# First attention of a two-layer transformer: where values and the output's last product stand in an iteration, and the order of the program's beginning

## The chip, the core and the metric

The kernel runs on one core of a Trainium2 chip. The core has five engines with a queue of instructions each: TensorE (PE; its loads of stationary operands are shown as PEld), VectorE (DVE), ScalarE (ACT), GpSimd (POOL) and SyncE (SP), which issues most DMAs. The metric is the device time of one execution in microseconds (us). The profile comes from one profiled execution; its span runs from the first to the last instruction.

## The reference

```python
x = x + xattn0(layernorm(x), fside, ctx, ctx)   # 16 heads of 8; 128 keys from fside, 120 from ctx
x = x + moe0(layernorm(x))                      # top 2 of 8 experts, silu
x = x + xattn1(layernorm(x), ctx, ctx)          # 16 heads of 8; 120 keys
x = x + moe1(layernorm(x))                      # top 2 of 8 experts, gelu
```

x is [64, 128, 128] in float32: 64 batches of 128 rows of width 128. An attention computes q, k and v with weights and biases, softmax(q k^T / sqrt(8)) v per head, and a product with the output weight. In the first one, the keys and values are 128 rows made from fside with the layer's weights, and 120 rows of ctx taken as they are. `moe0` makes its routing logits with a small attention over the eight experts' q, k, v.

## The kernel before

**Work and stages.** The 64 batches stay in SBUF as `xg`, in 16 groups of four (GB = 4). The program is: the first attention (to about 600 us), the first experts in 71 tiles of 256 tokens (to about 840), the second attention with the second experts beside it. The change is in the first attention and in what comes before it.

**An iteration of the first attention** (the loop in `attention`, from L482). It is a software pipeline: iteration `it` computes maxima for batch `it`, scores for batch `it - 2`, values and the first steps of the output for batch `it - 3`, and the last product for `it - 4`. Its parts, with the names used here:

- *Rounds* (`round_`, four per iteration, called in two pairs). Each has two maximum banks and two score banks of PSUM. A maximum bank (L344) is q k^T with queries on the partitions; DVE reduces it to the negated row maximum `nm` (L356). A score bank (L372) is k q^T; ACT takes its exponential into `p` (L380). The four matmuls of a bank pair use different groups of 32 rows of PE and run beside each other. A round issues the first half of all four banks, then the second.
- *Shift* (`shift`): PE transposes `nm` (L401), and DVE adds it to the queries (L404, two updates), so that scores come out with the maximum subtracted. Shift is for batch `it - 1`, and the next iteration's scores read the result.
- *Values* (`values`, L417): 32 matmuls p v into one bank, and `out1`, a copy of it by ACT (L426).
- *out2*: two transposes (L433), reciprocal of the sums (L437) and the product `o` (L439) on DVE. *out3*: a transpose (L446) and a copy on ACT (L448). *out4*: the product with wo (L453). *out5*: DVE adds to x (L458), and takes the statistics for the next normalisation (L113).
- *Preparation* (`prep`) of the group to come, spread over four iterations: queries (L269, and four ACT activations L273, two at each of the two places of `prep`), keys (L187, two activations L192), values (L199, DVE L206), and turning the normalised x (L165, ACT copy L166).
- *Router* (`aside.call`, twice in an iteration): small steps of the first experts' routing, on DVE (L655 to L806), PE, ACT and POOL, with the scatter DMAs of tokens on POOL (L754). Its `front` normalises a group on POOL (L156), turns it on PE and makes logits (L618), at times that `when` sets in iterations.
- *Lead* (`aside.ahead`): statistics of x for a group some ten batches ahead.

The order of a full iteration is: values and out1; DMA loads; rounds 0 and 1; out2; first part of preparation; rounds 2 and 3; shift; out3; router; out4 and out5; lead; second part of preparation; router.

**What sets the order.** The loop is recorded under `tc.manual_schedule`, so each engine executes in the order of the code. All PSUM tiles of this attention come from one pool of eight banks (`mtile`), so a new one waits until the last reader of an older one is done. What precedes the loop (constants, loads, first keys, values and queries) is recorded outside of it, in an order that a scheduler chooses. SP issues DMAs in order and waits at each for the one eight before.

**The beginning.** Four loads of x are issued first, then masks, the layer's weights, constants of the router, then fside's group 0 (`kvT`), the context's keys and values, and the other twelve loads of x. Group 0 is normalised on POOL and turned, and its queries are made for four batches at once.

Of the kernel before, what the change touches and what calls it, by code (L numbers as in the profile page):

```python
# [8 lines left out]
F32 = mybir.dt.float32  # L9
# [35 lines left out]
def transformer_kernel(ctx, tc, a, out):  # L45
# [16 lines left out]
    for g in range(4):  # L62
        load_x(g)
# [14 lines left out]
    def attention_weights(p):  # L78
        return dict(
            wq=load_const(p + "wq", [D, D], a[p + "wq"]),  # L80
            wk=load_const(p + "wk", [D, D], a[p + "wk"]),
            wv=load_const(p + "wv", [D, D], a[p + "wv"]),
            wo=load_const(p + "wo", [D, D], a[p + "wo"]),
            bq=load_const(p + "bq", [128, NS], a[p + "bq"]),
            bk=load_const(p + "bk", [128, NV], a[p + "bk"]),
            bv=load_row(p + "bv", D),
            bo=load_row(p + "bo", D),
        )

    hmask = load_const("hmask", [128, NS], a["hmask"])  # L90
    kmask = load_const("kmask", [128, NV], a["kmask"])
    smask = load_const("smask", [128, NV], a["smask"])
    l0 = attention_weights("a0_")
# [5 lines left out]
    class Norm:  # L99
# [6 lines left out]
        def stats(self, b):  # L106
            if self.n < 2:

                if b % GB == 0:
                    self.halves[b // GB] = stat.tile(  # L110
                        [S, GB, 6], F32, name=f"st{self.n}", tag=f"st{self.n}", bufs=3
                    )
                nc.vector.bn_stats(self.halves[b // GB][:, b % GB, :], xg[b // GB][:, b % GB, :])  # L113
                return
            st = stat.tile([S, 6], F32, name="st", tag="st")
            nc.vector.bn_stats(st, xg[b // GB][:, b % GB, :])
            nc.vector.bn_aggr(self.mv[:, b, :], st)  # L117

# [31 lines left out]
        def normed(self, g, pool=rows, bufs=1, width=D, xn=None, js=range(GB)):  # L150

            if xn is None:
                xn = pool.tile([S, GB, width], F32, name="xn", tag="xn", bufs=bufs)
            for j in js:
                b = g * GB + j
                nc.gpsimd.tensor_scalar(  # L156
                    xn[:, j, :D], xg[g][:, j, :], self.mv[:, b, 0:1], self.rstd[:, b : b + 1],
                    ALU.add, ALU.mult,
                )
            return xn  # L160
# [13 lines left out]
    for s in range(2):  # L174
        k = keep.tile([128, NV, GB, KF + KC], F32, name=f"k2_{s}", tag=f"k2_{s}")
        K2.append(k)
        v = keep.tile([KF, GB, H // 2, 2, 32], F32, name=f"v_{s}", tag=f"v_{s}")
        nc.gpsimd.memset(v, 0.0)
        for i in range(2):
            nc.gpsimd.memset(v[:, :, :, i, 16 * i + HD : 16 * i + HD + 1], 1.0)  # L180
        VS.append([v])
        m = keep.tile([S, 2, 128], F32, name=f"nm_{s}", tag=f"nm_{s}")
        nc.gpsimd.memset(m, 0.0)
        NM.append(m)
# [32 lines left out]
    def attention(layer, w, norm, first, aside):  # L217
# [5 lines left out]
        with ExitStack() as es:  # L223
# [18 lines left out]

            def context(g):
                if first:
                    s = g % 2
                    for v in range(NV):
                        nc.sync.dma_start(
                            k2[s][:, v, :, KF:], a["ctx_k"][:, v, g * GB : (g + 1) * GB, :]
                        )
                    nc.sync.dma_start(  # L250
                        vs[s][1].rearrange("k b h i w -> k b (h i w)"),
                        a["ctx_v"][:, g * GB : (g + 1) * GB, :],
                    )
# [49 lines left out]
            def prep(it, half):  # L303

                g, j = it // GB + 1, it % GB
                if not first:
                    if g == 1:
                        if (j, half) == (2, 1):
                            prep_v(1)
                        elif (j, half) == (1, 0):  # L310
                            prep_k(1)
                    elif g < NG:
                        pieces = (
                            (), (lambda: prep_k(g),),
                            (lambda: prep_v(g), lambda: prep_x(g)),
                            (lambda: prep_q(g, 0), lambda: prep_q(g, 1)),
                        )[j]
                        if half < len(pieces):
                            pieces[half]()
                    return  # L320
                if (it, half) == (0, 1):
                    norm_of(1)
                    prep_x(1)
                if (j, half) == (3, 1):
                    if g + 1 < NG:
                        prep_x(g + 1)
                elif g >= NG:
                    return
                elif j == 0 and it or it == 1:
                    prep_q(g, half)  # L330
                elif (j, half) == (2, 0):
                    prep_k(g)
                elif (j, half) == (2, 1):
                    prep_v(g)
# [126 lines left out]
            def norm_of(g):  # L461
                if g < NG:
                    normed[g] = norm.normed(g)

                    nc.gpsimd.tensor_tensor(
                        xg[g], xg[g], w["bo"].unsqueeze(1).to_broadcast([S, GB, D]), ALU.add
                    )

            if first:
                loads(0)  # L470
                context(0)
                yield
                norm_of(0)
                prep_k(0)
                prep_v(0)
                prep_x(0)
                prep_q(0, 0)
                prep_q(0, 1)
            else:
                prep_batch(0)  # L480
            loads(1)
            oTs, pos_ = {}, {}  # L482

            for it in range(B + (4 if first else 5)):
# [17 lines left out]
                on(3, lambda b: values(b, 0), lambda b: values(b, 1), out1)  # L502
# [3 lines left out]
                if it % GB == 2 and it // GB + 1 < NG:  # L506
                    context(it // GB + 1)
                rounds(0, 1)
                if first:

                    on(3, out2)
                    prep(it, 0)
                    rounds(2, 3)
                    on(1, shift)
                    on(3, out3)
                    aside.call(it, mtile)
                    on(4, out4, out5)
                    aside.ahead(it)
# [3 lines left out]
                else:  # L522

# [15 lines left out]
                    if it == 1:  # L539

                        nc.gpsimd.tensor_tensor(
                            xg[0], xg[0], w["bo"].unsqueeze(1).to_broadcast([S, GB, D]), ALU.add
                        )
# [18 lines left out]
    class Router:  # L562
# [5 lines left out]
        def __init__(self, pool, layer, norm, nlog, wr, logits, chosen, xnT_of, parts, when=(7.5, 8)):  # L568
# [145 lines left out]
    def logits1(rt, lg, n, l):  # L714
# [19 lines left out]

    spare = nc.sync.dma_start(
        xs[E * CAP - TT :].rearrange("(h p) d -> p h d", p=S),
        zero,
    )
    AFTER = mybir.DependencyInfo(mybir.DependencyClass.Sync, mybir.DependencyReason.DATA)
    DEEP = 4  # L740
    scatters = []
# [5 lines left out]
    def scatter(probe, j, k, xn):  # L747
# [11 lines left out]
        behind(s, [scatters[-DEEP] if len(scatters) >= DEEP else spare])  # L759
# [317 lines left out]
    class Aside0(Ahead):  # L1077
# [12 lines left out]

        def made(self, b):
# [17 lines left out]
    wr0 = load_const("wqkvT", [D, 3 * E], a["wqkvT"])  # L1109
# [3 lines left out]
    rp = ctx.enter_context(tc.tile_pool(name="route", bufs=1))  # L1113
    aside0 = Aside0()
    steps = attention(0, l0, norms[0], True, aside0)
    next(steps)
    for b in range(GB):
        aside0.lead(b)
    next(steps)
# [251 lines left out]
```

## Time and profile before

| | |
|---|---|
| three runs | 1531.78 us median, 1529.79 to 1535.51 |
| profiled execution | 1534.94 us, span 1533.1 us |
| mean granted TensorE clock | 0.976 |
| PE busy | 1415.5 us (92%) |
| DVE busy | 1057.7 us (69%) |
| ACT busy | 836.7 us (55%) |
| POOL busy | 641.6 us (42%) |
| first matmul of a round | 21.66 us |
| eight iterations, 195.19 to 268.59 us | 73.40 us |

A row of the timeline gives the start, the duration, engine, line, operation, output and inputs with their shapes and types, and a count when rows are merged; in brackets stands the idle time before it and what ended it. A row of the windows gives a stretch, its length, busy time and instructions of PE, PEld, DVE, ACT and POOL, the granted clock of PE as a share of full speed, the busy share of the DMA engines, and GB/s. A row of the waits gives who waited for whom: total us, times, longest. PE's ends are modelled, so time in which a block of matmuls waits inside counts as busy; distances between starts of blocks are safer.

### The profile page before, as it was taken

What the parts mean: (1) busy time and instruction counts of PE and PEld (TensorE: products, weight loads), DVE (VectorE), ACT (ScalarE), POOL (GpSimd) and SP (SyncE); (2) the same over time, 40 slices, a digit from 0 to 9 for tenths busy, and PEclk for the clock granted to TensorE, in tenths of its full rate; (3) what the DMA queues carried; (4) which work ended last, traced back from release to release, by engine and by line L of the source; (5) the groups of instructions that cost most, each with busy time, mean ns of one, the idle gap of its engine ahead of it and who ended that gap; (6) DMA issues with size and microseconds to landing.
All of it is one profiled execution on the core that took longest, in us unless ns stands there. A gap on an engine that the chain in (4) does not pass through costs nothing.

```text
span 1533.1 us, 44848 instructions
## 1 busy us (share of the span) xinstructions
PE 1415.5 (92%) x18156; PEld 1148.4 (75%) x18156; DVE 1057.7 (69%) x2923; ACT 836.7 (55%) x1722; POOL 641.6 (42%) x1211
## 2 busy tenths in 40 slices
PE   5999999999999999888999997579999999999988
PEld 3777777777777777777888887457787777777765
DVE  4777888888888986454544443458777767777763
ACT  3766666666666655433333332346666666656643
POOL 5123255656565635543000000677755565544110
PEclk9999999999999999999999999689999999999999
DMA  7421122222222221467766665111111111110000
GB/s 191 113 54 49 48 59 62 66 62 62 63 62 62 57 72 43 152 183 213 206 196 184 197 195 145 36 34 29 36 33 29 36 38 34 34 29 22 9 12 25
DMA packets 124130, 123.89 MB, mean 81 GB/s; under 512 B 47123, under 2 KB 106515, under 8 KB 122003
## 3 DMA queue, kind: packets, MB, share of 16 engines
q1 hardware_dynamic: 115730, 103.71, 24.8%
q0 software_dynamic: 8192, 17.32, 3.6%
q8 instruction: 143, 2.34, 0.6%
q14 instruction: 65, 0.52, 0.1%
HBM read 97.31 MB, written 23.67 MB: 79 GB/s over the span
## 4 chain that ended last, share of the span: by engine, by line
PE 67%; DVE 15%; POOL 6%; DMA 5%; ACT 4%; issue 3%; SPq 1%; POOLq 0%; ACTq 0%; DVEq 0%
PE bank L372 12%; PE bank L417 10%; PE bank L344 9%; PE bank L1000 9%; DVE nm L356 5%; PE bank L1228 4%; PE bank L1249 3%; PE bank L1013 3%; DMA q<-xs 2%; DMA vc<-xs 2%; PE bank L433 2%; DVE q L404 2%; PE bank L618 2%; PE bank L187 2%; DVE h L1243 2%
## 5 line engine op out<-in xcount | busy, mean ns | idle before, releaser
L356 DVE TENSOR_REDUCE nm<-bank 128x2 f32<-128x496 f32 (+1 forms) x768 | 461.9, 662 | 105.9 <-PE bank L372 74.2
L372 PE MATMUL bank<-q,k 32*120 32x256 f32 (+1 forms) x3072 | 452.3, 406 | 7.2 <-DVE q L404 4.4
L380 ACT ACTIVATE p<-bank 120x512 f32<-120x512 f32 (+1 forms) x768 | 401.1, 602 | 105.2 <-PE bank L372 70.4
L344 PE MATMUL bank<-k,q 32*128 32x248 f32 (+1 forms) x4096 | 449.1, 340 | 2.4 <-ACT q L298 1.1
L344 PEld LDWEIGHTS bank<-k,q 32*128 32x128 f32 x4096 | 347.4, 188 | 63.7 <-issue 21.7
L372 PEld LDWEIGHTS bank<-q,k 32*120 32x120 f32 (+1 forms) x3072 | 291.4, 181 | 36.6 <-DVE nm L356 17.0
L1005 DVE TENSOR_TENSOR p<-p,bank 128x256 f32<-128x256 f32 x213 | 88.4, 420 | 134.1 <-ACT p L1004 134.1
L417 PE MATMUL bank<-p,v 128*32 128x128 f32 (+1 forms) x4096 | 177.9, 279 | 0.1
L754 POOL DMA_INDIRECT xs<-xn,at x128 | 128.8, 1006 | 52.8 <-issue 29.5
L1160 POOL DMA_INDIRECT yb<-ys,back x128 | 123.7, 967 | 32.5 <-issue 25.7
L1004 ACT ACTIVATE p<-bank 128x256 f32<-128x256 f32 x213 | 81.0, 383 | 100.7 <-PE bank L1000 100.2
L426 ACT COPY ov<-bank 128x256 f32<-128x256 f32 x128 | 47.8, 373 | 158.7 <-PE bank L417 158.7
L417 PEld LDWEIGHTS bank<-p,v 128*32 128x32 f32 (+1 forms) x4096 | 110.3, 110 | 20.3 <-issue 12.3
L1000 PE MATMUL bank<-q 128*128 128x256 f32 x516 | 118.6, 379 | 1.8 <-ACT q L991 1.8
L404 DVE SCALAR_TENSOR_TENSOR q<-bank,c_smask,q 128x256 f32<-128x256 f32 x256 | 111.2, 476 | 11.8 <-PE bank L401 9.0
L156 POOL TENSOR_SCALAR xn<-x,mv,rstd 128x128 f32<-128x128 f32 x256 | 111.2, 447 | 11.6 <-PE bank L165 5.7
L273 ACT ACTIVATE q<-bank,c_a_bq,c_hmask 128x512 f32<-128x512 f32 x124 | 89.7, 780 | 29.0 <-PE bank L269 29.0
L417 PE MATMUL bank<-p,vc 120*32 120x128 f32 x2048 | 104.6, 274 | 0.3 <-issue 0.3
L1000 PEld LDWEIGHTS bank<-q 128*128 128x128 f32 x516 | 94.7, 190 | 13.2 <-ACT q L991 2.1
L1146 POOL MEMSET gates<- 128x256 f32 x2 | 0.6, 312 | 248.4 <-DMA ys<-q 248.4
L144 POOL TENSOR_SCALAR rstd<-mv 128x4 f32<-128x4 f32 (+1 forms) x33 | 6.5, 197 | 202.7 <-DVE mv L117 113.7
L1000 PE MATMUL bank<-vc 128*128 128x256 f32 x336 | 78.8, 385 | 0.0
(201 smaller groups left out, 2271.1 us busy)
## 6 DMA issues: line engine op xcount, KB each, us to landing
q<-in_w SPq DMA_DIRECT2D x43, 576.0 KB, 4.4
vc<-in_w SPq DMA_DIRECT2D x28, 576.0 KB, 4.1
vc<-in_ctx_v SPq DMA_DIRECT2D x16, 960.0 KB, 7.0
k<-in_ctx_k SPq DMA_DIRECT2D x32, 240.0 KB, 2.9
q<-xs SPq DMA_DIRECT2D x43, 128.0 KB, 2.2
ys<-q SPq DMA_DIRECT2D x43, 128.0 KB, 2.3
x<-in_x SPq DMA_DIRECT2D x16, 256.0 KB, 7.8
kvT<-in_fsideT SPq DMA_DIRECT2D x16, 256.0 KB, 2.7
```

Of the source, the lines that this page charges most:

```text
L156: nc.gpsimd.tensor_scalar(xn[:, j, :D], xg[g][:, j, :], self.mv[:, b, 0:1], self.rstd[:, b : b + 1], ALU.add, ALU.mult,)
L273: nc.scalar.activation(q4s[g][:, :, s, :], pq.rearrange("p (b q) -> p b q", b=GB), AF.Identity, bias=w["bq"][:, s : s + 1], scale=hmask[:, ...
L344: nc.tensor.matmul(pa[:, u, :], lhsT=q4s[g][r, j, s, :], rhs=k2[g % 2][r, s // 2, j, :], start=True, stop=True,)
L356: nc.vector.tensor_reduce(nm[b % 2].rearrange("q i (a s) -> q a i s", s=16)[:, 2 * ra + v : 2 * ra + v + len(slots) // 2, :, 0], pa.rearra ...
L372: nc.tensor.matmul(pb[:n, v * 256 : (v + 1) * 256], lhsT=k2[g % 2][r, v, j, k0 : k0 + n], rhs=q4s[g][r, j, 2 * v : 2 * v + 2, :].rearrange ...
L380: nc.scalar.activation(ps_[b][:n, c, ra, :], pb[:n], AF.Exp, scale=SCALE)
L404: nc.vector.scalar_tensor_tensor(q, pm, smask[:, v : v + 1], q, ALU.mult, ALU.add)
L417: nc.tensor.matmul(pav[32 * ra : 32 * ra + 32, v * S : (v + 1) * S], lhsT=vs[g % 2][c][:, j, 4 * v + ra, i, :], rhs=p[:n, c, ra, (2 * v + ...
L754: s = nc.gpsimd.indirect_dma_start(xs, bass.IndirectOffsetOnAxis(at[:, j, k : k + 1], 0), xn, None)
L1000: nc.tensor.matmul(ph[:, u, :], lhsT=w[:, c, u * 128 : (u + 1) * 128], rhs=xT, start=True, stop=True)
L1005: nc.vector.tensor_tensor(hT[:, c, :], sa, ph[:, 1, :], ALU.mult)
L1160: nc.gpsimd.indirect_dma_start(y[:, k, b % 2, :], None, ys, bass.IndirectOffsetOnAxis(back[:, b, k : k + 1], 0),)
```

## The change

1. In the first attention, values and out1 stand between rounds 0, 1 and rounds 2, 3, followed by the context's loads, out4 and out5 (now for batch `it - 5`), lead and the router's first call. After rounds 2 and 3 come shift, out3 (now for `it - 4`), out2, both parts of preparation, and the router's second call. The loop has one iteration more.
2. Queries of a group are made with both parts of preparation next to each other. For group 0 they are made batch by batch (`prep_batch`), the later ones inside the first iterations; the values of group 0 and the queries of group 1 move into the loop as well.
3. The beginning is recorded under a manual schedule with SP. Loads are issued in the order in which they are used: x of group 0, wk, bk, kmask, `kvT`, wq, bq, hmask, the context's keys, wv, bv, smask, x of group 1, the context's values, and so on. Group 0 is normalised by DVE (`alone`).
4. The router normalises a group at 8 and turns it at 9 iterations after the group's first (7.5 and 8 before). `xn` gets two buffers.

```diff
-    for g in range(4):
-        load_x(g)
+    begin = ctx.enter_context(ExitStack())
+    begin.enter_context(tc.manual_schedule(engines=ORDERED | {ET.SP}))
+    load_x(0)
...
+        def alone(self, b0, b1, xn):
+            for b in range(b0, b1):
+                st = stat.tile([S, 6], F32, name="st", tag="st")
+                nc.vector.bn_stats(st, xg[b // GB][:, b % GB, :])
+                nc.vector.bn_aggr(self.mv[:, b, :], st)
+            r = self.rstd[:, b0:b1]
+            nc.vector.tensor_scalar(r, self.mv[:, b0:b1, 1], EPS, None, ALU.add)
+            nc.gpsimd.tensor_tensor(r, r, power.to_broadcast([S, b1 - b0]), ALU.pow)
+            for b in range(b0, b1):
+                nc.vector.tensor_scalar(
+                    xn[:, b % GB, :], xg[b // GB][:, b % GB, :], self.mv[:, b, 0:1],
+                    self.rstd[:, b : b + 1], ALU.subtract, ALU.mult,
+                )
...
+                if half == 0 and it < GB - 1:
+                    prep_batch(it + 1)
                 if (it, half) == (0, 1):
+                    prep_v(0)
                     norm_of(1)
+                if (it, half) == (1, 1):
+                    biased(0)
+                if (it, half) == (2, 1):
                     prep_x(1)
+                if (it, half) == (3, 0):
+                    prep_q(1, 0)
+                    prep_q(1, 1)
...
-            for it in range(B + (4 if first else 5)):
+            for it in range(B + 5):
...
-                on(3, lambda b: values(b, 0), lambda b: values(b, 1), out1)
...
-                rounds(0, 1)
+                vals = (lambda b: values(b, 0), lambda b: values(b, 1), out1)
                 if first:
-
+                    rounds(0, 1)
+                    on(3, *vals)
+                    if it % GB == 2 and it // GB + 1 < NG:
+                        context(it // GB + 1)
+                    on(5, out4, out5)
+                    aside.ahead(it)
+                    aside.call(it, mtile)
+                    rounds(2, 3)
+                    on(1, shift)
+                    on(4, out3)
                     on(3, out2)
                     prep(it, 0)
-                    rounds(2, 3)
-                    on(1, shift)
-                    on(3, out3)
-                    aside.call(it, mtile)
-                    on(4, out4, out5)
-                    aside.ahead(it)
                     prep(it, 1)
                     aside.call(it, mtile)
                     aside.end(it, work, mtile)
                 else:
+                    on(3, *vals)
+                    rounds(0, 1)
...
-parts, when=(7.5, 8)):
+parts, when=(8, 9)):
...
+    steps = attention(0, l0, norms[0], True, aside0)
+    next(steps)
+    l0.update(attention_weights("a0_", ("wq", "bq")))
+    hmask = load_const("hmask", [128, NS], a["hmask"])
+    next(steps)
+    l0.update(attention_weights("a0_", ("wv", "bv")))
+    smask = load_const("smask", [128, NV], a["smask"])
+    load_x(1)
+    next(steps)
+    l0.update(attention_weights("a0_", ("wo", "bo")))
+    for g in range(2, 4):
+        load_x(g)
...
+    aside0.begin()
+    zeros_and_ones(VS[1][0])
     next(steps)
+    begin.close()
```

## The prediction

> **What bounds it now.** The page first: PE is busy all through the first attention, yet a busy share hides waits between matmuls, so I read one iteration in order of time.
>
> ```profile
> span 1533.1 us, 44848 instructions
> ```
>
> PE's timeline in an iteration without other work; each row is the first matmul of a block:
>
> ```profile
> 207.46 0.47 PE L344 MATMUL bank<-k,q 32*128 32x248 f32 x1
> ...
> 209.38 0.44 PE L433 MATMUL bank<-ident,ov 128*128 128x128 f32 x2
> ...
> 209.75 0.47 PE L344 MATMUL bank<-k,q 32*128 32x248 f32 x1
> ...
> 212.68 0.44 PE L401 MATMUL bank<-ident,nm 128*128 128x128 f32 x2
> ...
> 213.06 0.39 PE L453 MATMUL bank<-c_a_wo,oT 128*128 128x128 f32 x2
> 213.38 0.43 PE L417 MATMUL bank<-p,v 128*32 128x128 f32 x8
> ```
>
> Rounds 0 and 1 take 1.92 us (207.46 to 209.38); rounds 2 and 3, the same work, take 2.93. The missing 1.0 us is in DVE's timeline:
>
> ```profile
> 208.60 2.42 DVE L356 TENSOR_REDUCE nm<-bank 128x2 f32<-128x496 f32 x4 [1.82 <-PE bank L372]
> 210.94 0.25 DVE L437 RECIPROCAL rs<-bank 128x16 f32<-128x16 f32 x1
> ...
> 211.43 2.41 DVE L356 TENSOR_REDUCE nm<-bank 128x2 f32<-128x496 f32 x4
> ...
> 213.75 0.87 DVE L404 SCALAR_TENSOR_TENSOR q<-bank,c_smask,q 128x256 f32<-128x256 f32 x2
> 214.53 0.28 DVE L458 TENSOR_TENSOR x<-x,bank 128x128 f32<-128x128 f32 x1
> 214.85 0.49 DVE L113 BATCH_NORM_STATS2 st<-x 128x6 f32<-128x128 f32 x2
> ```
>
> Reduces follow each other every 0.58 us (208.60 to 210.94 for four), slower than the rounds fill banks. The last bank of round 3 is out2's, free when DVE has made o at 211.51: 1.17 before shift's transposes at 212.68. So a bank freed late for a score costs some 1.0 us (its two matmuls share a row group, 0.48 each). The first reduce comes 1.14 after a round starts (208.60 - 207.46). Other steps, start to start: values 1.90, out2 0.37, shift 0.27, out3 0.11, out4 0.32; sum 7.81. A cycle of eight iterations, which holds all of preparation and router, in the windows' sum row:
>
> ```profile
> sum 73.40, PE 71.74 PEld 56.11 DVE 63.30 ACT 48.49 POOL 42.62; mean PE 8.97 PEld 7.01 DVE 7.91 ACT 6.06 POOL 5.33
> ```
>
> 9.18 us an iteration, with DVE busy 7.91 of it: DVE is nearly the bound too.
>
> **The change, step by step.** The changed order on PE: rounds 0,1; values; out4; [router's turn]; rounds 2,3; shift; out3; out2; preparation. On DVE: four reduces; out5 and two statistics; router's first call; four reduces; shift's two updates; reciprocal and o; preparation's v; router's second call. Time 0 is the start of rounds 2,3.
>
> (a) *The bank wait goes.* The other four reduces end while values run: rounds 2,3 take 1.92, a gain of 1.0.
>
> (b) *A new wait.* The next rounds' first score reads q after shift's update, and values no longer stand between. DVE: reduces 1.14 to 3.47, first update, and 0.53 from its start to PE (32.43 to PE's 32.96 at the loop's beginning): scores at 4.0. PE is past out2 at 2.82 (shift 1.92, out3, out2 at 2.45 because its bank waits for the second reduce). Rounds to 5.91, values to 7.81, out4 to 8.13. So the plain iteration is 8.13 against 7.81: this wait takes back all of (a) and 0.32 more.
>
> (c) *Preparation hides in that wait*, and no longer adds: turning x 0.5 (8.13 in all); keys and values 2.0 end at 4.82, so 8.95 against 9.29.
>
> (d) *Queries.* Before, their four activations run in two pairs with exponentials between:
>
> ```profile
> 200.09 1.44 ACT L273 ACTIVATE q<-bank,c_a_bq,c_hmask 128x512 f32<-128x512 f32 x2
> 201.43 2.29 ACT L380 ACTIVATE p<-bank 120x512 f32<-120x512 f32 x4
> ...
> 204.41 1.45 ACT L273 ACTIVATE q<-bank,c_a_bq,c_hmask 128x512 f32<-128x512 f32 x2
> ```
>
> After, both pairs stand together (4 x 0.695 = 2.78), and the built order has round 1's last score waiting for their bank. Matmul 2.82, +1.06 to ACT, +2.78: free at 6.7; that score and its partner 1.0, values and out4 2.22: 9.94, where (b)'s wait alone would have given 8.13.
>
> Two plain or turning, one (c), one (d): 35.15 per four, 70.3 per eight.
>
> (e) *Router on DVE.* Out5 needs out4 (done 8.2, seen 8.38), then 0.32 and 0.40: DVE is free at 9.10, and the reduces of rounds 2,3 are ready at 9.27. Only 0.17 of cover: what the first call holds on DVE beyond that makes the reduces late, so the updates, so the scores. By the rows of L655 to L806 (some 0.25 a step, 0.6 for the three wide reduces) the first calls of eight iterations, from the queries' one on, hold 0.6, 1.0, 1.0, 0.75, 1.1, 1.5, 0, 0. The router's turning of x (0.53, first call of the iteration after the queries) now lies bare between out4 and rounds: it lengthens that stretch twice in eight and covers as much of DVE. Late by: 0.43, 0.30, 0.83, 0.58, 0.93, 0.80, 0, 0. The second call has 0.45 of cover (DVE free at 4.74; values start at 5.91 and need a bank that the first reduce frees 0.72 after its start); its work goes beyond in four: 0.9 (a copy of logits behind three steps frees round 1's last bank at 6.1), 0.1, 0.24, 0.16. Base, lateness, second call and turning together: 9.94 + 0.43 + 0.53 = 10.90; 8.13 + 0.30 + 0.89 = 9.32; 8.95 + 0.83 = 9.78; 8.13 + 0.58 + 0.11 = 8.82; 9.94 + 0.93 + 0.53 = 11.40; 8.13 + 0.80 = 8.93; 8.95 + 0.24 = 9.19; 8.13 + 0.16 = 8.29. Sum 76.6. (The wait of the router's small matmuls for ACT, 0.45 each, goes: they lie in the new wait.) Against 73.4 that is **+3.2 per eight**. The router runs for 54 iterations: +22; the first eight without it by 35.15 against 34.1 per four (10.37 less 1.6 of router, 7.82, 9.29, 8.25): +2.
>
> (f) *The beginning.* Waits, and the timeline:
>
> ```profile
> PE bank L187 <- DMA kvT<-in_fsideT: 14.8, 1, 14.8
> ```
>
> ```profile
> 23.12 9.39 DVE L356 TENSOR_REDUCE nm<-bank 128x2 f32<-128x496 f32 x16 [3.72 <-PE bank L344]
> ...
> 32.43 0.86 DVE L404 SCALAR_TENSOR_TENSOR q<-bank,c_smask,q 128x256 f32<-128x256 f32 x2
> ```
>
> kvT is issued behind twenty others, at 10.88, and landed 3.9 later. As fifth it goes out at 2.7 (0.74 + 0.52 + 3 x 0.47): landed 6.6. Keys 2.05, their two activations 1.45, a copy and the query matmul 0.7, one short activation (no row; 0.27 by the copy of that size, at most the 0.7 of the wide one), +1.5 to the first reduce: 12.7, against 23.12. But DVE then does 8 statistics and v between the reduces (2.4): update at 24.4 against 32.43, **-8**. Group 1's context stands behind twelve x loads on SP's queue, issued at 38.80 both ways since the same bytes precede it; needed at some 43 now instead of 52, landed 2.9 later, at 41.7: no stall, up to 3 if it slips.
>
> (g) *The end.* Before, by the chain, PE waits for the last normalisation but one on POOL:
>
> ```profile
> 602.81 1.75 POOL xn L156 x4
> ...
> 604.60 0.34 PE bank L165
> ```
>
> and then runs at half clock to 612. Turning now comes an iteration after the statistics: the 4.7 of POOL's chain lies under work. **-4** (0 to -6): 1.7 of idle and 3 of slow clock, less an iteration's tail of out3 to out5, which lies under the expert tiles. The second attention's order is unchanged: 0.
>
> **A rule against it.** TensorE's clock in the windows:
>
> ```profile
> 31.00:33.00 2.00, 0.04 (x4) 0.04 (x4) 2.00 (x5) 0.15 (x1) 0.00 (x0) 0.77 1.16 283
> 33.00:35.00 2.00, 2.00 (x20) 1.84 (x24) 1.75 (x6) 0.00 (x0) 0.82 (x5) 0.50 0.27 50
> ```
>
> A PE idle for 2.4 us got half clock for 6 us, a loss of 3; bank waits of 1.0 in each iteration left it at 1.00 from 40 to 600. The Trainium skill ("TensorE: Matmul & The Clock Gate", "A second HAM failure mode: psum-queue depth-cycling") says that a PE pausing on banks between groups can swing between the clocks. The new pauses are 1.2 plain and some 1.5 in (d). By the row: 0. By the rule, once per group of four: 16 x 3 = 48. I take the row, since the pauses stay under 2.4.
>
> **Sum.** +22 +2 -8 -4 = +12. The profiled execution took 1534.94 (span 1533.1, 1.8 around it), 3 above the median of 1531.78. 1547 by the one, 1544 by the other; I give **1544**.
>
> **Rivals.** *A, as above* (0.52): 1534 to 1558, by 0.2 us either way per iteration. *B, faster* (0.22): DVE's cover in (e) is longer than 0.17 (statistics shorter, out5 seen sooner), so the router costs only its turning: 70.3 + 1.1 = 71.4, -2.0 per eight, -13; with (f) and (g) -25: 1507. For it: DVE's total of 63.3 leaves room. Against it: order on DVE is fixed and out5 waits for out4. It decides below 75.0 per eight. *C, a wash* (0.14): half of (e), 74 to 75.5; 1531. *D, worse* (0.12): the rule above holds, or DVE stands at router steps that POOL has not fed (its scatters take 1.0 each): +30 to +48, 1562 to 1580. That the change does nothing can't be: the order differs on each engine.
>
> **Numbers.** A's lower edge lies within 0.5% (7.7 us, about what a measurement here can tell): 0.06 of its 0.52. So slower 0.46 + 0.12 = 0.58, same 0.14 + 0.06 = 0.20, faster 0.22. The range of 8 in 10 reaches into B and D: 1509 to 1566.
>
> **What would show it.** Rounds 2,3 in 1.9 (a); PE waiting on L433, the changed kernel's update, ahead of rounds 0, some 1.2 us (b); round 1's last score waiting for ACT's queries once in four iterations, 1.5 us or more (d); first reduce at 12 to 13 (f); no PE wait on POOL near 600 (g); eight iterations in 76 to 77. Wrong if the update comes before PE is done with out2, or if the granted clock leaves 1.00 between 40 and 600.

## The result, and the profile after

| | before | after |
|---|---|---|
| median of 8 runs each, side by side | 1534.3 us (1529.79 to 1535.51) | 1540.14 us (1538.39 to 1544.39) |
| ratio, 95% interval | 1 | 1.0049 (1.0034 to 1.0064) |
| span of the profiled execution | 1533.1 us | 1536.6 us |
| mean granted clock | 0.976 | 0.978 |
| eight iterations with router | 73.64 us | 75.67 us |
| the eight with the router's lists (shift of batch 48 to 56) | 75.4 us | 79.7 us |

The changed kernel is slower by half a per cent, 5.8 us by the medians and 3.5 by the profiled spans. The 73.40 us of eight iterations, from which the prediction counted, began at the second row of a block of values (195.19) and ended at the first row of another (268.59). The first row of the block is this one in the kernel before:

```profile
194.94 0.42 PE L417 MATMUL bank<-p,v 128*32 128x128 f32 x8
```

From first row to first row it is 73.65 us; the 73.64 of the table goes by the starts of shift. The page:

```profile
span 1536.6 us, 44811 instructions
```

PE's timeline of the changed kernel in an iteration without other work, each row the first of a block (start, duration, engine, line, operation, operands, idle before and what ended it):

```profile
58.53 0.47 PE L373 MATMUL bank<-k,q 32*128 32x248 f32 x1
...
60.44 0.44 PE L430 MATMUL bank<-ident,nm 128*128 128x128 f32 x2
60.72 0.27 PE L475 MATMUL bank<-ident,o 128*128 128x128 f32 x1
60.98 0.44 PE L462 MATMUL bank<-ident,ov 128*128 128x128 f32 x2
...
62.53 0.48 PE L401 MATMUL bank<-q,k 32*128 32x256 f32 x1 [0.51 <-DVE q L433]
...
64.53 0.43 PE L446 MATMUL bank<-p,v 128*32 128x128 f32 x8
...
66.43 0.49 PE L482 MATMUL bank<-c_a_wo,oT 128*128 128x128 f32 x2
66.85 0.47 PE L373 MATMUL bank<-k,q 32*128 32x248 f32 x1
```

Rounds 2 and 3 now take 1.91 us (58.53 to 60.44), where they took 2.93. Then PE has done out2 and two maximum matmuls, and stands: its next score (62.53) needs shift's update. The whole iteration takes 8.32 (58.53 to 66.85). DVE's timeline in the same stretch:

```profile
59.67 2.42 DVE L385 TENSOR_REDUCE nm<-bank 128x2 f32<-128x496 f32 x4 [0.15 <-PE bank L401]
62.01 0.86 DVE L433 SCALAR_TENSOR_TENSOR q<-bank,c_smask,q 128x256 f32<-128x256 f32 x2
...
63.32 2.48 DVE L385 TENSOR_REDUCE nm<-bank 128x2 f32<-128x496 f32 x4
66.96 0.29 DVE L487 TENSOR_TENSOR x<-x,bank 128x128 f32<-128x128 f32 x1 [1.17 <-PE bank L482]
67.28 0.49 DVE L109 BATCH_NORM_STATS2 st<-x 128x6 f32<-128x128 f32 x2
67.99 2.42 DVE L385 TENSOR_REDUCE nm<-bank 128x2 f32<-128x496 f32 x4 [0.22 <-PE bank L401]
```

The update starts at 62.01, 0.52 before the score that reads it. At the other end DVE stands for 1.17 us, because its next instruction in order, the addition to x, wants out4, which PE reaches only after the values. When it is done only 0.22 are left before the next reduces. So DVE has its free time while values run, and none where the router's first call stands. The waits of the loop (who waited for whom: us in total, times, longest; 100 to 500 us) of the changed kernel:

```profile
DVE x L487 <- PE bank L482: 46.8, 42, 1.5
```

and of the kernel before, whose largest wait of DVE was for the maxima themselves, that is, for PE:

```profile
DVE nm L356 <- PE bank L372: 48.5, 62, 2.7
```

What PE itself waited for in the changed kernel (90 to 480 us):

```profile
PE bank L401 <- ACT q L293: 10.7, 11, 1.0
PE bank L430 <- DVE nm L385: 7.1, 21, 0.5
```

The first is once in each group of four, the queries' bank. The second is shift, waiting for reduces that the router's first call made late. One eight of the router in the windows (stretch, length, busy time of PE, PEld, DVE, ACT, POOL, granted clock, DMA share, GB/s):

```profile
167.27:243.04 75.77, 71.49 (x1142) 55.76 (x1141) 63.56 (x163) 48.68 (x98) 33.92 (x79) 1.00 0.21 55
```

DVE's work is what it was (63.56 against 63.30), PE's too (71.49 and 71.74), and 2 us were added to the time in which each of them stands. The beginning:

```profile
5.53 2.05 PE L202 MATMUL bank<-kvT,c_a_wk 128*128 128x512 f32 x2 [5.53 <-DMA kvT<-in_fsideT]
...
24.71 0.72 PE L401 MATMUL bank<-q,k 32*128 32x256 f32 x1 [2.10 <-DVE q L433]
```

```profile
12.66 2.42 DVE L385 TENSOR_REDUCE nm<-bank 128x2 f32<-128x496 f32 x4 [3.04 <-PE bank L373]
...
24.18 0.86 DVE L433 SCALAR_TENSOR_TENSOR q<-bank,c_smask,q 128x256 f32<-128x256 f32 x2
```

The first update comes at 24.18 instead of 32.43. The end, as a row of the windows from the kernel before and then from the changed one:

```profile
606.00:612.00 6.00, 6.00 (x80) 5.24 (x83) 0.75 (x4) 0.37 (x1) 3.47 (x7) 0.50 0.15 49
```

```profile
606.00:612.00 6.00, 4.79 (x99) 3.78 (x98) 3.46 (x10) 3.04 (x7) 1.50 (x3) 1.00 0.01 3
```

The granted clock (third figure from the end) is 1.00 instead of 0.50, and PE has no wait for POOL near 600.

Inside the loop the clock fell once, in the eight with the router's lists. The lists' steps on DVE (498.50 to 500.84) stand ahead of the reduces and make them late, and after the longest wait of PE between 45 and 600 us the granted clock is 0.50 for 3.4 us (to 506.1); in the kernel before it stays at 1.00 from 39 to 605 us:

```profile
501.48 0.33 PE L475 MATMUL bank<-ident,o 128*128 128x128 f32 x1 [1.47 <-DVE nm L385]
```

```profile
500.00:502.00 2.00, 0.53 (x4) 0.31 (x3) 1.97 (x5) 1.01 (x3) 1.81 (x3) 1.00 0.00 0
502.00:504.00 2.00, 1.97 (x7) 0.81 (x10) 2.00 (x6) 0.57 (x2) 1.82 (x6) 0.67 0.02 4
504.00:506.00 2.00, 2.00 (x22) 1.92 (x17) 1.48 (x8) 2.00 (x4) 1.82 (x3) 0.50 0.11 39
```

**The ledger.** Starts of shift's transposes, changed kernel less the kernel before: batch 4: -6.7; batch 8: -6.6; batch 16: -5.7; then +2.0 to +2.1 in each of four eights: +2.5 at batch 48; +4.4 in the eight with the lists: +6.9; last batch: +9.8. The last values lie +3.8, the first expert tile +3.8, the span +3.5. So the beginning gave 6.7, the loop took 16.4, the end gave 6.0.

### The profile page after: what moved, and what is told of

Same layout as the page of the kernel before. It is cut to its first block, busy times and chain, and to the rows that moved or that the text cites. A ratio compares the mean times of both kernels' runs of the same rounds, so it can differ in the third digit from the quotient of the medians.

```text
span 1536.6 us, 44811 instructions
## 1 busy us (share of the span) xinstructions
PE 1411.3 (92%) x18162; PEld 1143.2 (74%) x18162; DVE 1064.3 (69%) x2935; ACT 842.7 (55%) x1739; POOL 642.2 (42%) x1198
## 4 chain that ended last, share of the span: by engine, by line
PE 62%; DVE 20%; ACT 6%; POOL 4%; DMA 4%; issue 3%; SPq 0%; POOLq 0%; DVEq 0%; ACTq 0%
PE bank L446 10%; PE bank L1029 9%; PE bank L401 8%; PE bank L373 7%; DVE nm L385 6%; PE bank L1283 4%; PE bank L1042 3%; PE bank L1304 3%; ACT q L293 3%; DVE q L433 2%; PE bank L482 2%; DMA q<-xs 2%; DMA vc<-xs 2%; PE bank L202 2%; PE bank L462 2%
## 5 line engine op out<-in xcount | busy, mean ns | idle before, releaser
L401 PE MATMUL bank<-q,k 32*120 32x256 f32 (+1 forms) x3072 | 417.3, 404 | 21.8 <-ACT q L293 12.7
L373 PEld LDWEIGHTS bank<-k,q 32*128 32x128 f32 x4096 | 351.0, 191 | 47.7 <-DVE nm L385 11.9
L401 PEld LDWEIGHTS bank<-q,k 32*120 32x120 f32 (+1 forms) x3072 | 277.7, 181 | 43.0 <-ACT q L293 18.2
L433 DVE SCALAR_TENSOR_TENSOR q<-bank,c_smask,q 128x256 f32<-128x256 f32 x256 | 111.2, 476 | 10.7 <-PE bank L430 8.1
L293 ACT ACTIVATE q<-bank,c_a_bq,c_hmask 128x512 f32<-128x512 f32 x120 | 85.4, 780 | 34.2 <-PE bank L289 34.2
L487 DVE TENSOR_TENSOR x<-x,bank 128x128 f32<-128x128 f32 x128 | 36.2, 282 | 71.8 <-PE bank L482 70.3
```

The costliest lines, as they stand in the source:

```text
L293: nc.scalar.activation(q4s[g][:, :, s, :], pq.rearrange("p (b q) -> p b q", b=GB), AF.Identity, bias=w["bq"][:, s : s + 1], scale=hmask[:, ...
L373: nc.tensor.matmul(pa[:, u, :], lhsT=q4s[g][r, j, s, :], rhs=k2[g % 2][r, s // 2, j, :], start=True, stop=True,)
L401: nc.tensor.matmul(pb[:n, v * 256 : (v + 1) * 256], lhsT=k2[g % 2][r, v, j, k0 : k0 + n], rhs=q4s[g][r, j, 2 * v : 2 * v + 2, :].rearrange ...
L433: nc.vector.scalar_tensor_tensor(q, pm, smask[:, v : v + 1], q, ALU.mult, ALU.add)
```

## Experiments

Twelve measurements were made in three sets, each on one chip and beside the kernel before: 1532.99 us in the first set, 1618.59 in the second, 1631.2 in the third. The chips of the second and third set grant TensorE less clock in the second attention (0.92 between 1100 and 1500 us, against 1.00), so only ratios to the kernel before are compared between sets.

| kernel | set | ratio, 95% interval | us per eight with router |
|---|---|---|---|
| new beginning alone | 1 | 0.9963 (0.9949 to 0.9978) | 73.6 |
| new loop alone | 1 | 1.0097 (1.0081 to 1.0114) | 75.6 |
| values first | 1 | 1.0003 (0.9991 to 1.0014) | 75.3 |
| router before out4, at 8.5 and 9.5 | 1 | 1.0019 (1.001 to 1.0028) | 76.2 |
| router before out4, at 9 and 10 | 2 | 1.0036 (1.0023 to 1.005) | 76.5 to 78.1 |
| queries by batch | 2 | 1.0062 (1.0039 to 1.0084) | 76.6 to 77.6 |
| queries by batch, router before out4 | 2 | 1.0003 (0.9989 to 1.0018) | 75.3 to 78.4 |
| out2 before shift | 2 | 1.0201 (1.0168 to 1.0233) | 78.1 to 82.5 |
| the changed kernel again | 3 | 1.0046 (1.0026 to 1.0066) | 77.1 |
| new order in four iterations, then the old | 3 | 0.9965 (0.9951 to 0.9979) | 75.9 to 77.9 |
| values first, router before out4 | 3 | 1.0018 (1.001 to 1.0026) | 77.1 to 78.9 |
| queries by batch, router before out4, again | 3 | 1.0008 (0.9996 to 1.0021) | 75.4 to 79.0 |

The part behind the first attention has the same order in all kernels, yet it is not equally long in every execution: from the first expert tile to the end it took 912.6 to 919.7 us in the traces of the kernel before, the changed kernel and the four of the first set. The start of the first expert tile leaves it out: 617.5 us in the kernel before, 621.3 in the changed one, 614.0 with the new beginning alone, 626.8 with the new loop alone, 615.7 with values first, 622.1 with the router before out4. These are single executions.

### The two halves apart

New beginning, old loop (edit of the changed kernel, its core):

```diff
-                    rounds(0, 1)
                     on(3, *vals)
...
+                    rounds(0, 1)
                     on(3, out2)
                     prep(it, 0)
                     rounds(2, 3)
                     on(1, shift)
+                    on(3, out3)
+                    aside.call(it, mtile)
+                    on(4, out4, out5)
+                    aside.ahead(it)
...
-parts, when=(8, 9)):
+parts, when=(7.5, 8)):
```

> The changed kernel's beginning with the old order of the loop. Ledger theory: the beginning is worth 8.2 us at the first update of queries (24.71 against 32.96 in the traces) and the early iterations give back little, so some 1526 us, 8 below before; the cycle of eight stays at 73.4. Rival (the gain of the beginning is lost anyway, because the context of group 1 and the x loads come no earlier): 1534.

Measured: 1528.35 us, ratio 0.9963. And the opposite, the old beginning with the new loop (out4 and out5 for `it - 5`, one iteration more):

> The changed order of the loop, and the router's later times, with the old beginning. Ledger theory: +15 over the loop and -6 at its end leave some +9 to +13 over before, 1543 to 1547, with 75.7 per eight iterations. Rival (the loop is even and the time is lost in the early iterations that take over group 0's preparation): 1534.

Measured: 1547.89 us, ratio 1.0097; eight iterations in 75.6. So the loop's order loses some 15 us by itself and the beginning gains by itself, and the product of both, 1.006, is near the 1.0049 of the whole. But the beginning alone gave 4.6 us, not 8. PE's timeline of this kernel shows where 5 of its 8 went:

```profile
30.95 0.80 PE L316 MATMUL bank<-xnT,c_a_wq 128*128 128x128 f32 x2 [0.96 <-ACT xnT L314]
36.24 0.44 PE L430 MATMUL bank<-ident,nm 128*128 128x128 f32 x2
...
45.92 0.47 PE L401 MATMUL bank<-q,k 32*120 32x256 f32 x1 [1.24 <-ACT q L293]
```

In the old order a batch's preparation stands between rounds 0, 1 and rounds 2, 3, and PE waits there for ACT, in iterations that are already full of it: shift of batch 1 is at 36.24 here and at 30.76 in the changed kernel. In the new order this work lies where PE waits for the update anyway. The two halves of the change lean on each other in these four iterations, and only there.

### The new order for four iterations only

```diff
+                if first and it >= GB:
+                    on(3, *vals)
+                    rounds(0, 1)
+                    if it == GB:
+                        on(4, out3)
+                        on(5, out4, out5)
+                    on(3, out2)
+                    prep(it, 0)
+                    rounds(2, 3)
+                    on(1, shift)
+                    on(3, out3)
...
-                if first:
+                elif first:
                     rounds(0, 1)
```

> The new beginning and the new order for iterations 0 to 3 only, then the old order with the router's old places. Theory: the beginning's 8.2 us are kept where the first four iterations run in the new order (the changed kernel's shift was 8.8 us ahead at iteration 4, the old order under the new beginning only 3.5), and from there the old order's 73.6 us per eight iterations with router: ratio 0.9955 (some 6.7 us less), loop 73.6 per eight, shifts 6 to 7 us ahead of the kernel before throughout. Rival: the 5 us that the old order lost in iterations 1 to 3 are lost a little later when the order is switched, because what was lost is the preparation's work and not its place: then 0.9965 to 0.998, as with the new beginning alone (0.9963).

Measured: 0.9965 (0.9951 to 0.9979). Both forecasts lie in the interval, so the totals do not tell the theory from its rival. By the trace it is 3.7 us ahead of the new beginning alone from batch 8 to batch 16 (95.9 and 167.9 us, against 99.6 and 171.6), but that is on another chip. It is 0.8% below the changed kernel of the same set, and no better by its ratio than the new beginning alone. These two are the versions that beat both kernels.

### Which of the loop's two new waits costs

Step (b) of the prediction (the update has no cover) and step (e) (router's first call late) are each taken away by moving one block. Values back ahead of rounds 0 and 1, so that they cover the update:

```diff
-                    rounds(0, 1)
                     on(3, *vals)
...
+                    rounds(0, 1)
                     on(5, out4, out5)
```

> The changed kernel with values back ahead of rounds 0,1; everything else as changed. Theory: the update is hidden again (plain iteration 7.8), but preparation (3.5 per four), the router's turning and its first calls on DVE (6 per eight) lie bare, because the bank of shift's transposes waits for the first reduce of rounds 2,3: 77 per eight, 1540 to 1555, no better than the changed kernel. Rival (values in the middle are what costs, by the new wait for the update): 73.4 per eight or less, 1525 or less.

Measured: ratio 1.0003, eight in 75.3. Neither forecast. The update's wait is gone and iterations without router gain: batch 8 is 2.7 us ahead of the changed kernel's (93.8 against 96.5). With router nearly all of it is lost again. PE no longer waits for the update or the queries' bank, but for shift's reduces instead (90 to 480 us; 7.1 in the changed kernel):

```profile
PE bank L430 <- DVE nm L385: 19.1, 27, 1.0
```

PE's timeline and DVE's, with the router at work:

```profile
204.08 0.44 PE L430 MATMUL bank<-ident,nm 128*128 128x128 f32 x2 [0.97 <-DVE nm L385]
```

```profile
201.38 0.28 DVE L487 TENSOR_TENSOR x<-x,bank 128x128 f32<-128x128 f32 x1
201.69 0.49 DVE L109 BATCH_NORM_STATS2 st<-x 128x6 f32<-128x128 f32 x2
202.09 0.26 DVE L830 TENSOR_TENSOR one<-one,row 128x64 f32<-128x64 f32 x1
...
203.28 0.17 DVE L833 CAST at<-posns 128x8 int32<-128x8 f32 x1
203.36 2.41 DVE L385 TENSOR_REDUCE nm<-bank 128x2 f32<-128x496 f32 x4
```

The two sets of reduces now stand close together, and everything on DVE between them, output and router (201.38 to 203.36), makes shift's transposes late by 0.97. What the values no longer cover here, they covered in the changed kernel.

The router's first call ahead of out4 and out5, into the gap in which DVE waits for out4; this needs the router half an iteration later, or a whole one:

```diff
+                    aside.call(it, mtile)
                     on(5, out4, out5)
                     aside.ahead(it)
-                    aside.call(it, mtile)
...
-parts, when=(8, 9)):
+parts, when=(8.5, 9.5)):
```

> The changed kernel with the router's first call ahead of out4 and out5, where DVE stands 1.1 us an iteration waiting for out4; its normalising and turning move half an iteration later so that the statistics are there. Theory: the first calls' steps fit into that idle time and no longer make the reduces late: 73 to 73.7 per eight, 15 us less, 1525. Rival (DVE's steps there cost nothing now, since DVE has slack): no change, 1540.

Measured: ratio 1.0019, eight in 76.2, no gain in the plain eights. The eight with the lists gained: 76.3 instead of 79.7, and the granted clock did not fall there. Over the whole first attention it comes out even (first expert tile at 622.1, against 621.3), so this trace does not explain the better ratio. The half iteration moved the router's longest steps into the second call, where DVE's timeline has them before the reduces of rounds 0 and 1:

```profile
210.57 0.29 DVE L832 TENSOR_TENSOR one<-one,row 128x64 f32<-128x64 f32 x1
...
212.01 0.90 DVE L835 CAST at<-posns 128x8 int32<-128x8 f32 x1
212.83 2.40 DVE L385 TENSOR_REDUCE nm<-bank 128x2 f32<-128x496 f32 x4
```

```profile
213.54 0.42 PE L446 MATMUL bank<-p,v 128*32 128x128 f32 x8 [1.65 <-DVE nm L385]
```

Values wait 1.65 us for the bank that these reduces free. Here the case for the first call was confounded by the second. With a whole iteration of delay (`when=(9, 10)`) the steps keep their halves:

> As router_before, but with normalising and turning moved by a whole iteration (9 and 10), so that each of the router's steps stays in the call it had in the changed kernel; in router_before the longest one (two products, two sums, two casts, 2.2 us) had come to stand in the second call, ahead of the reduces of rounds 0,1. Theory: the first calls now fit into DVE's wait for out4, and nothing is added to the second ones: 73.4 to 74 per eight against 75.7, some 13 us less than the changed kernel, 1526. Rival (DVE's total decides, and not the place): 75.7 to 76.2, 1537 to 1540.

Measured: ratio 1.0036, eight in 76.5 to 78.1, on a chip where the changed kernel's own are not known from that set (77.1 in the third). Against the 1.0049 of the changed kernel the interval allows 0 to 4 us, where 2 us in each of seven eights had been expected. PE's wait for shift's reduces is gone from its trace, as the theory had it, but another has come, which was 1.0 us in the changed kernel:

```profile
PE bank L401 <- DVE q L433: 6.6, 20, 0.5
```

With 1.5 us of waits of the values for reduces that is some 8 us of waits of PE for DVE between 90 and 480 us, as in the changed kernel (7.1 and 1.0).

Both edits at once:

> The changed kernel with both single edits at once: values ahead of rounds 0 and 1 again (alone: ratio 1.0003), and the router's first call ahead of output's last product, an iteration later (alone: 1.0019 and 1.0036). Theory, that the place of the values and what is queued behind the router's steps are two separate costs of the new order: they add, 1.0049 - 0.0046 - 0.002 = 0.998 (0.9965 to 0.9995), some 74 us per eight. Rival, that both edits free the same wait (DVE's reduces and update late behind the router's steps): no better than values first alone, 1.0003 (0.9995 to 1.0015), 75.3 per eight.

Measured: 1.0018, with the changed kernel at 1.0046 beside it. They do not add: it is no better than values first alone in the first set. Its DVE timeline:

```profile
252.39 0.25 DVE L654 COPY lg<-bank 128x96 f32<-128x96 f32 x1
256.34 2.42 DVE L385 TENSOR_REDUCE nm<-bank 128x2 f32<-128x496 f32 x4 [3.70 <-PE bank L401]
258.67 0.22 DVE L687 TENSOR_TENSOR eq<-rest,m 128x64 f32<-128x64 f32 x1
```

DVE is idle for 3.70 us ahead of one set of reduces, and does the router between the two sets. Shift waits little for it now (0.9 us in all between 90 and 480 us). What comes late is the addition to x, which stands behind the router's steps (259.58), and PE's loads for the scores wait for the bank that it frees:

```profile
PEld bank L401 <- DVE x L487: 11.9, 25, 0.9
```

With values first, a place for the router ahead of values might be better than the one between; that was not run.

### The update's wait made larger

To see whether the update is on the path at all, out3 and out2 go ahead of shift, so that o delays it on DVE:

```diff
-                    on(1, shift)
                     on(4, out3)
                     on(3, out2)
+                    on(1, shift)
```

> The changed kernel with out3 and out2 ahead of shift on PE and DVE: reciprocal and o (0.49 us on DVE) come before the updates of the queries. Theory of step (b): the update is on the path in plain and turning iterations, which become 0.4 to 0.5 longer (PE covers it in the iteration with keys and values, the queries' bank in theirs): 2 per eight more, some +13, 1553. Rival (the update is hidden, and the reduces' banks set the time): no change, 1540.

Measured: ratio 1.0201, 1.5% above the changed kernel's. PE now stands twice as long for it:

```profile
64.23 0.48 PE L401 MATMUL bank<-q,k 32*128 32x256 f32 x1 [0.99 <-DVE q L433]
```

The update is on the path. Before the router's main steps on DVE begin, and at a clock of 1.00, the times from update to update compare with those of the changed kernel in the third set: 8.81 against 8.31 in an iteration with nothing to prepare, 8.98 in both with keys and values, 10.44 in both with queries, which is what the theory named. The loss is larger than the 13 us expected. Eights with router take 78.1 where the clock stays at 1.00, 1 more than the 77.1 of the third set, and 82.5 where it falls (last section); what else was late was not worked out.

### The queries' bank

```diff
+                if half == 0 and it >= GB and g < NG:
+                    prep_q_one(g, j)
...
-                elif j == 0 and it:
-                    prep_q(g, half)
```

`prep_q_one` makes the queries of one batch: one matmul of 128 columns and four short activations, in each of the four iterations.

> The changed kernel with the queries of a group made batch by batch, one in each of four iterations, by a 128-column product and four activations of 128 columns into the same places: no PSUM bank is held for four wide activations. Theory of step (d): the queries' iteration falls from 9.9 to the 8.4 of the others, 3.0 per eight less, 72.7; over 15 groups 22 us less, 1518. Rival (ACT, which gets 6.0 instead of 2.8 us of activations per group, delays exponentials in every iteration): no gain, 1540 or more.

Measured: ratio 1.0062. PE's wait for ACT (the 10.7 us shown above) is gone from this kernel, and the time did not fall. Before the router's main steps on DVE begin, the iteration with queries took 8.8 us instead of the 10.4 of the third set, but two others grew by 0.4 and 0.6: 35.5 instead of 36.2 for four, where 1.5 had been expected. With router nothing is left of that (77.5 against 77.1). Together with the router before out4:

> q_by_batch and router_before_9 together. Theory: the two costs are in different iterations and add: 70.5 to 71 per eight, 35 us less than the changed kernel, 1505, and faster than both kernels. Rival: DVE (63.6 busy of 75.7) becomes the bound, and the sum is less than its parts, 1518.

Measured: 1.0003. Since the changed kernel had not run on that chip, it was repeated beside it:

> The order with the queries batch by batch and the router's first call ahead of output's last product, run again beside the changed kernel itself: on the other chip it took 1.0003 of the kernel before, against 1.0049 of the changed kernel on an undisturbed one. Theory, that the two edits together take back some 7 us of the loop whatever the chip: 0.996 to 1.0005 below or at the kernel before, and 0.4 to 0.7 per cent below the changed kernel beside it. Rival, that it was the chip: within 0.2 per cent of the changed kernel beside it.

> The changed kernel itself, beside the three others on one chip. Expected ratio to the kernel before 1.005 (1.003 to 1.007), as first measured. Its trace also tells whether the waits inside the values' matmuls for nothing the profile shows (0.9 us and 0.7 us in about every group, seen in four kernels on the slower chip) belong to the chip or to those four orders: if the chip on which this runs is an undisturbed one and they are absent here and in the q_and_router order too, they belonged to the chip.

Measured: 1.0008 and 1.0046. So the two edits together do take back 0.4% on the same chip, the lower edge of what the theory gave, though its absolute ratio was missed. Most of it is not where it was looked for. The plain eights are no shorter (79.0 against 77.1, with stalls of that chip in both); the eight with the router's lists took 79.1 instead of 84.3 us, and in it the granted clock fell to 0.50 for 3.4 us in the changed kernel and not in this one.

## Why the prediction was right, and by how much its steps were off

The sign, the mechanism and the likeliest case held: predicted 1544 us, measured 1540.14, in case A (eight iterations above 75.0). The total is nearer than its sum. Forecast was +12, measured +5.8 by the medians. It was added to 1531.78, the median of three runs; beside the changed kernel the kernel before took 1534.3, and these 2.5 us are luck. Two of the signs did not come out: eight iterations took 75.67, not 76 to 77, which is nearer to the upper edge of case C (75.5) than to the forecast of 76.6; and the clock left 1.00 once.

- **(a)** Rounds 2 and 3 in 1.92: measured 1.91. With the router's first call they are longer, 2.44 in one case (shift at 197.43 us, PE 0.46 idle for the reduces).
- **(b)** Update at 3.47 and scores at 4.0 after rounds 2: measured 3.48 and 4.00; PE is past out2 at 2.82, as forecast. The iteration is 8.32, not 8.13: out4 takes 0.42 with its gap instead of 0.32, and rounds 0, 1 take 2.00 instead of 1.91. The kernel with out2 first shows that this wait sets the time.
- **(c), (d)** Keys and values 8.95 forecast, 8.98 measured; turning 8.13 and 8.32; queries 9.94 and 9.90. The wait for the queries' bank is 1.0, not the 1.5 or more that was named as its sign.
- **(e)** The eight in the order given there: 10.71, 9.26, 9.56, 8.79, 11.02, 8.92, 9.04, 8.37, sum 75.67 against 76.63. This is the term that was mis-sized. Without router the four iterations make 35.52 (twice 8.32, 8.98, 9.90), so the router adds 4.6 per eight, where 6.3 had been worked out, while the eight without it take 71.04, 0.7 above the forecast: two errors that partly cancel. Another 0.25 of the +3.2 was the short count of the kernel before (73.40 for 73.65). The step's "+22" came out as +15.5, and 2.3 of these belong to the eight with the router's lists, whose own steps on DVE it did not count: there the update starts 3.51 after shift's transposes instead of 1.60. The "+2" of the eights without router was +1.
- **(f)** First reduce at 12.66 (12.7), update at 24.18 (24.4), first score 8.25 earlier. That the first number agrees is in part luck: kvT had landed at 5.53, not 6.6, and the steps from there to the first reduce took 7.1 instead of 6.1. 1.6 of the gain went back by batch 4: net -6.7. No stall for the context's loads. That the gain hangs on the new loop order in the first iterations was not in the prediction.
- **(g)** -6.0 instead of -4; the new loop alone shows it too (last update +15.3, first expert tile +9.3). PE's idle for POOL and the half clock are both gone.
- **The clock.** The row was taken against the Trainium skill ("TensorE: Matmul & The Clock Gate", "A second HAM failure mode: psum-queue depth-cycling"). From 40 to 500 us the changed kernel bore it out: 1.00, with 0.5 to 1.0 us of waits in every iteration. Then the sign of being wrong came, for 3.4 us. It can have cost 1.7 us at most (an estimate, half of the 3.4); the values of that iteration start 4.41 us after the update, against 4.21 in the same iteration of an earlier eight. The reason given, that pauses under 2.4 us are safe, does not hold: the pause ahead of this fall was 1.47, and see below.

The sum had +12; the spans have +3.5: 7.6 less lost in the loop and 2.0 more gained at the end, but 1.3 less gained at the beginning.

Rival B fell because the cover behind out5 really is small (0.22 in the row above, 0.17 forecast). What the experiments do not settle is a repair: with each of the single edits the router's DVE steps only went to another place where one of the two sets of reduces was waiting. It was shown that such a step costs; whether a third place would be free remains open.

## What to carry to other kernels

Taking away a bank wait gains only if what follows is not fed by the same engine: here 1.0 us of PE's wait became a wait for DVE's update, because the block that had covered that update was used to cover the reduces. When a shared engine is near its limit (DVE 7.9 of 9.2 us), put the free work where that engine idles in order, and look what stands first in its queue: DVE idled for 1.1 us in each iteration with router work queued behind one addition. And split a change into its halves before judging it: this one held a gain of 0.4% and a loss of 1%.

## What the runs showed of the hardware that was not expected

**Half clock after short pauses.** In the kernel with out2 first (second set) the windows show the granted clock fall in the middle of the loop:

```profile
254.00:256.00 2.00, 1.72 (x16) 1.33 (x18) 1.93 (x7) 0.14 (x1) 1.65 (x5) 0.96 0.75 213
256.00:258.00 2.00, 2.00 (x23) 1.97 (x22) 1.80 (x5) 0.71 (x2) 1.95 (x4) 0.50 0.20 70
...
266.00:268.00 2.00, 1.98 (x4) 1.15 (x5) 1.97 (x6) 0.13 (x1) 0.00 (x0) 0.52 1.03 229
```

The longest idle of PE in the 20 us around is 0.84 us, and it comes after the first fall (a block that waits inside counts as busy, so pauses can be hidden). A drop of 3.4 us comes twice within 14 us, and so again 160 us later. The chip alone does not bring it: the three other kernels of the set show none between 52 and 500 us. Pauses of 0.3 to 0.8 us preceded it here. In the changed kernel single waits as long left 1.00 until 500 us, and one of 1.47 preceded the fall there; with the router before out4 (first set) four waits of 1.65 to 1.70 us left the clock at 1.00. So the length of one pause does not decide. A swing between two clocks is what the cited section describes; which pattern of pauses brings it was not worked out.

**The same kernel, other stalls on another chip.** In the changed kernel, values take 1.97 us in every iteration of the first measurement. In the third set, in one of eight iterations, they took 3.22:

```profile
224.00 0.40 PE L446 MATMUL bank<-p,v 128*32 128x128 f32 x7
224.71 0.28 PE L446 MATMUL bank<-p,v 128*32 128x128 f32 x1 [0.31 <-issue]
...
225.44 0.43 PE L446 MATMUL bank<-p,vc 120*32 120x128 f32 x5 [0.33 <-issue]
```

"issue" means that PE waited for nothing that the profile shows. It makes 77.1 of 75.7 us per eight for the same program, and more in other orders (14 such rows between 90 and 480 us in the kernel with the old order, 8 in this one). That PE's instructions come late is a guess; it was not tested. The ratio to the kernel before was the same on both chips, 1.0049 and 1.0046.
